# A gated cross-attention and mixture-of-experts kernel on one core: surplus branch in mid-stream, k of two batches at once, routing table in thirds

## The chip, the cores and the metric

The kernel runs on one core of a Trainium2 chip. The metric is the device time of one execution in microseconds (us), lower is better, as the median of several runs. All arithmetic is in 32-bit floats.

The core has five engines that each take their own instructions in order and meet over semaphores: PE (TensorE, matrix products; its weight loads are listed apart as PEld), DVE (VectorE), ACT (ScalarE), POOL (GpSimd) and SP (SyncE, which here only starts transfers). A "q" behind an engine's name (POOLq, PEldq) marks steps of its sequencer: branches, semaphores, register loads, drains.

## What is computed

Eight batches of 256 tokens with 256 features go through gated cross-attention (16 heads of 64, context of 120 rows) and then a gated mixture of eight experts of which each token takes two. Cut to what matters:

```python
x = x + tanh(g_xattn) * attention(layernorm(x), context)   # B=8, N=256, D=256, M=120
x = x + tanh(g_ffn) * moe(layernorm(x))

def attention(x, context):
    q = x @ w_q                      # 256 -> 16 heads x 64
    k, v = split(context @ w_kv)     # 256 -> 2 x 1024
    p = softmax(q @ k.T / 8)         # per head
    return (p @ v) @ w_out + b_out

def moe(x):                          # E=8 experts, DFF=1024
    probs = softmax(x @ Wr.T)
    top2 values, divided by their sum, are the gates
    return sum over the two experts e of gate_e * (silu(x @ W1[e].T) @ W2[e].T)
```

## The kernel before, in words

The order of instructions on PE, DVE, ACT and SP is written by hand: they are issued as the program's text runs (`tc.manual_schedule`), and each engine takes its own in that order. POOL does small arithmetic and the indirect transfers. Everything is one long straight stream with one branch at its end.

**Attention stage.** The loop runs over 32 units `(b, o, nb)`: a batch, one half of the heads, one half of the tokens; `k = 2*o + nb` counts the four units of a batch. In unit `s` PE takes, in this order: `scores` of the next unit (tile psc; DVE takes its maximum mx, ACT the exponentials pr), `weigh` (tile po, probabilities times v; in k=0 and k=2), `logits` (tile plT, and pl after it; the router's input, in k=1 of the odd batches from 3 on), one `project_q` for the next batch (pq), `project_k` (pk; k=1 and k=3), `wide_out` (pw; the output projection; k=1 for the first half of the batch before, k=2 for the second), `project_v` (pv; k=0 and k=3), and `turn_pr` (tr, the transposes of the unit's probabilities, which ACT copies into `pT_sb` and `weigh` reads). On DVE the copy of pk into kT comes first, then `divide` (probabilities by their sums) of the next unit, then the `router` (maximum, exponential on ACT, two picks, tally), then the sums of `wide_out`.

`project_k` makes k of one batch in two halves of four column blocks. Each matmul takes 120 columns of the context (one batch). psc has a single buffer; the projections share four PSUM buffers (`ps_mm`).

Two batches form a group of 512 tokens for routing. Each routed token's row (256 normalised features, its gates, its number) is sent by POOL's indirect transfers (L362) into a list per expert in DRAM, `routed`.

**Expert stage.** Tiles of 128 rows of one expert's list. First come eight tiles that are known to exist (`first`, one per expert, order 0, 1, 2, 6, 3, 4, 5, 7), then 23 `full` tiles whose expert and row are looked up in a table, and in steps 16 to 23 two `quad` tiles beside them, which mix the last rows of four experts. In step `i` PE does `go_up` of tile i (ph: 16 matmuls, ACT's SiLU behind it), the transposes of tile i+1 (`turn`, xtT, copied by DVE into xT), and `down` of tile i-1 (py: 8 matmuls; each 32-bit matmul has two records in the profile, and a weight load for each). DVE scales py by the gate into y (L856), and POOL adds y to the output by an indirect transfer (L873), each held until the one before has landed. For full tiles DVE also copies the expert's weights (L803, L812). SP loads rows four tiles ahead (L771, L791).

The last batch's output projection and routing lie in steps 1 to 4: `norm_y` and `norms_y.finish` (rows, L193), then `turn_y` (lnT_f, L203) at the head of step 2.

`table()` is a generator of small DVE steps on rows of up to 31 numbers: it finds for each full tile its row and expert (`full_row`, `expert_i`; L673 to L702), and then the same for quads (L705 to L751). It is run in two pieces, at the ends of steps 4 and 5:

```python
        if i == 4:
            parts = table()
            ...
        if 3 < i < 6:
            tables.append(next(parts))
```

**The branch.** The lists could be longer than 23 full and two quad tiles; for that the program ends with a conditional body (L1216 loads a count into a register of each engine, L1217 branches on it). For these inputs the count is zero and the body is jumped over.

The prologue (L119 to L165) makes constants on DVE and POOL, among them three for the table (`quarter_i`, `lane`, `places_q`; L140 to L151), while PE runs eleven idle matmuls (L1019).

Of the kernel before, what the change touches and what calls it, by code (L numbers as in the profile page):

```python
# [9 lines left out]
F32 = mybir.dt.float32  # L10
I32 = mybir.dt.int32
AF = mybir.ActivationFunctionType
ALU = mybir.AluOpType
AX = mybir.AxisListType

P = 128
B, N, D = 8, 256, 256
M = 120
# [8 lines left out]
DC = D // P  # L27
# [21 lines left out]
def tile_gated_xattn_moe(  # L49
# [74 lines left out]
    for e in range(E):  # L124
# [12 lines left out]
        places_q[:, QUADS:], [[1, 4 * QUADS]], base=0, channel_multiplier=0,  # L137
        allow_small_or_imprecise_dtypes=True,
    )
    quarter_i = const.tile([P, 1], I32, name="quarter_i")  # L140
    nc.vector.tensor_scalar(
        quarter_i, number[:, 0:1], 5, None, ALU.arith_shift_right
    )
    lane = const.tile([P, 1], F32, name="lane")
    nc.vector.scalar_tensor_tensor(
        lane, quarter_i, float(-QUARTER), number[:, 0:1], ALU.mult, ALU.add
    )
    for q in range(QUADS):
        nc.vector.tensor_scalar(
            places_q[:, q : q + 1], quarter_i, float(4 * q), None, ALU.add  # L150
        )  # L151
    octal = const.tile([P, E], F32, name="octal")
    for e in range(E):
        nc.vector.memset(octal[:, e : e + 1], float(E**e))
# [8 lines left out]

    minus_half = const.tile([P, 4], F32, name="minus_half")
    nc.gpsimd.memset(minus_half, -0.5)  # L165

    class Norms:

# [291 lines left out]

    kTs = {}

    def project_k(b, h):
        if h == 0:
            kTs[b] = ap.tile([P, IC, M], F32, tag="kT", name=f"kT_{b}")
        pk = ps_mm.tile([P, 512], F32, tag="mm", name=f"pk_{b}_{h}")
        for i in range(4):
            for c in range(DC):
                nc.tensor.matmul(
                    pk[:, ts(i, M)],  # L470
                    lhsT=wkv_sb[:, c, ts(4 * h + i, P)],
                    rhs=ctxT_sb[:, c, ts(b, M)],
                    start=(c == 0),
                    stop=(c == DC - 1),
                )
        return lambda: nc.vector.tensor_copy(
            kTs[b][:, ts(h, 4), :].rearrange("p c m -> p (c m)"), pk[:, : 4 * M]
        )

    def project_q(b, xnT, h):  # L480
# [188 lines left out]
    def table():  # L669

        rest_i = row("rest_i", E, I32)  # L673
        nc.vector.scalar_tensor_tensor(
            rest_i, count(NBLK, fw[2]), float(-P), bump, ALU.add, ALU.add
        )
        whole_i = row("whole_i", E, I32)
        nc.vector.tensor_scalar(whole_i, rest_i, 7, None, ALU.arith_shift_right)
        counts, begin = row("counts", 2 * E), row("begin", 2 * E)
        tails, whole = counts[:, :E], counts[:, E:]  # L680
        nc.vector.tensor_scalar(whole, whole_i, 1.0, None, ALU.mult)
        left = row("left", E)
        nc.vector.scalar_tensor_tensor(
            left, whole, float(-P), rest_i, ALU.mult, ALU.add
        )
        nc.vector.tensor_scalar(tails, left, float(P - QUARTER), None, ALU.is_gt)
        nc.vector.tensor_scalar(begin[:, E:], first_row, float(P), None, ALU.add)
        nc.vector.scalar_tensor_tensor(
            begin[:, :E], whole, float(P), begin[:, E:], ALU.mult, ALU.add
        )  # L690
        upto = summed("w", counts)

        at = row("at", FULLS)
        nc.vector.tensor_scalar(at, places_w, upto[:, 2 * E - 1 :], None, ALU.add)
        used = row("used_w", FULLS)
        nc.vector.tensor_scalar(used, at, 0.0, None, ALU.is_ge)
        which, first = sought("w", at, upto, counts, begin, P)
        full_row = row("full_row", FULLS, I32)
        where(first, used, full_row)
        expert_i = row("expert_i", FULLS, I32)  # L700
        nc.vector.tensor_scalar(used, which, float(E), float(-E), ALU.is_ge, ALU.mult)
        nc.vector.tensor_tensor(expert_i, which, used, ALU.add)  # L702
        yield expert_i, full_row

        quarters = row("quarters", E)  # L705
        nc.vector.tensor_scalar(quarters, left, 0.0, None, ALU.is_gt)
        for k in range(1, 3):
            nc.vector.scalar_tensor_tensor(
                quarters, left, float(k * QUARTER), quarters, ALU.is_gt, ALU.add
            )  # L710
        nc.vector.scalar_tensor_tensor(
            quarters, tails, -3.0, quarters, ALU.mult, ALU.add
        )
        upto_q = summed("q", quarters)
        used = row("used_q", 5 * QUADS)
        nc.vector.tensor_scalar(used, places_q, upto_q[:, E - 1 :], None, ALU.is_lt)
        which, first = sought("q", places_q, upto_q, quarters, begin[:, :E], QUARTER)
        where(first, used, first)
        nc.vector.tensor_scalar(which, which, float(E - 1), None, ALU.min)

        quad_row = row("quad_row", QUADS, I32)
        nc.vector.tensor_scalar(quad_row, first[:, :QUADS], lane, None, ALU.add)
        own = row("own", QUADS * E).rearrange("p (n e) -> p n e", e=E)
        eighth = row("eighth", QUADS)
        nc.vector.tensor_scalar(
            eighth, which[:, :QUADS], -1.0, float(E), ALU.mult, ALU.add
        )
        shape = [P, QUADS, E]
        nc.vector.tensor_tensor(
            own,  # L730
            rank.unsqueeze(1).to_broadcast(shape),
            eighth.unsqueeze(2).to_broadcast(shape),
            ALU.is_equal,
        )
        octets = which[:, QUADS:].rearrange("p (n e) -> p n e", e=E)
        nc.vector.tensor_tensor(
            octets, octets, octal.unsqueeze(1).to_broadcast([P, QUADS // 2, E]), ALU.mult
        )
        experts_i = row("experts_i", QUADS // 2, I32)
        with nc.allow_low_precision("whole numbers under 2**24, exact"):  # L740
            nc.vector.tensor_reduce(experts_i, octets, AX.X, ALU.add)

        more, more_i = row("more", 1), row("more_i", 1, I32)
        nc.vector.tensor_scalar(
            more, upto[:, 2 * E - 1 :], float(SPARE - FULLS), 0.0, ALU.add, ALU.max
        )
        more_q = row("more_q", 1)
        nc.vector.tensor_scalar(
            more_q, upto_q[:, E - 1 :], float(-4 * MIXED), 0.0, ALU.add, ALU.max
        )  # L750
        nc.vector.tensor_tensor(more_i, more, more_q, ALU.add)  # L751
        yield quad_row, own, experts_i, more_i
# [283 lines left out]
    for s, (b, o, nb) in enumerate(units):  # L1036
# [32 lines left out]
        elif n < B:  # L1069
            project_q(n, xnTs[n], k - 1)  # L1070
        if k == 1:
            if n < B:
                copies.append(project_k(n, 0))
            if routing and n < B:
                lg = next(lg)
            if b > 0:
                sums.append(wide_out(b - 1, 0, ps_mm))
            if routing and n == B:
                lg = next(lg)
        if k == 3:  # L1080
            if n < B:
                copies.append(project_k(n, 1))
            if b > 0:
                project_v(b, 1)
        for copy in copies:
            copy()
        if s + 1 < len(units):
# [13 lines left out]
        if n < B:  # L1101
            for step, each in list(sending.items()):
                if s < 8 * step + 18:
                    next(each)
        if b == 0 and k == 2:
            nc.vector.tensor_scalar(bias_sb, bias_sb, tg[:, 0:1], None, ALU.mult)
        if s in (3, 4):
# [34 lines left out]
    load_expert(5)  # L1142
    g = NG - 1
    for i, t in enumerate(order):
        w2_of = state["ready"][2][2]
        if i == 2:
            turn_y(B - 1, bank_tr)
# [22 lines left out]
            open_tile(order[i + 1], xts[i + 1])  # L1170
        if mixed:
            next(running)
        if i == 0:
            norms_y.finish()
            weigh(B - 1, 1, ps_py)
# [3 lines left out]
        if i == 3:  # L1179
            sending[g] = places(g, groups[g][0], picked[g], bank_tr)  # L1180
        w2 = w2_of()
        close_tile()
        state["pending"] = *new, w2
        if mixed:
            next(running)
        if i == 1:
            norms_y.finish()
        if i == 2:
            lg = next(lg)
            picked[g] = router(g, lg)  # L1190
# [5 lines left out]
                next(sending[g])  # L1196
        if i == 4:
            parts = table()
            routing_pool.close()
            qp.append(  # L1200
                ctx.enter_context(
                    tc.tile_pool(name="quads", bufs=1, side="right", reuse_waits="tile")
                )
            )
        if 3 < i < 6:
            tables.append(next(parts))
        while len(xts) <= min(i + AHEAD, len(order) - 1 if tables else 7):
            xts[len(xts)] = load(order[len(xts)])
# [3 lines left out]
            load_expert(3)  # L1212
            load_expert(7)
    close_tile()

    more = nc.values_load(tables[1][3][0:1, 0:1], min_val=0, max_val=FULLS)  # L1216
    with tc.If(more > 0):  # L1217
        spare = {}
        for j in range(SPARE):
            tj = ("full", j)  # L1220
            xt = load(tj)
            w1, gate, copy_w2 = weights(tj, xt)
            w2 = copy_w2()
            down(tj, up(tj, turn(tj, xt), w1), gate, xt, w2)
        for j in range(MIXED, QUADS):
            for _ in quad(j, load(("quad", j))):
                pass
        spare = None


# [41 lines left out]
```

## Time and profile before

| | |
|---|---|
| median of 3 runs | 548.06 us (547.97 to 548.73) |
| the profiled execution | 547.79 us; its span 546.0 us |
| mean granted PE clock | 0.991 |
| PE busy | 527.7 us (97% of the span) |
| DVE, ACT, POOL busy | 285.8, 219.5, 129.3 us |
| attention stage, to the first tile (PE, L832) | to 274.3 us |
| first tiles, last batch's routing, table | to about 336 us |
| full and quad tiles | to 531.8 us |
| tail, PE's last matmul to the end | 531.8 to 546.0 us |

Times below are microseconds from the span's start in that one execution. In the profile's lists an operation is named by line, engine and "output <- inputs"; "idle before <- releaser" says what ended the idle time of the engine ahead of it.

### The profile page before, as it was taken

Reading aid. Unit: us, or ns where it says so; the run is one execution under the profiler, and the core shown is the slowest. Engines: PE = TensorE matmul, PEld = TensorE weight load, DVE = VectorE, ACT = ScalarE, POOL = GpSimd, SP = SyncE. Lnnn points to the kernel's source line nnn. Section 1 sums busy time; section 2 is a strip of 40 time slices with the busy share of each in tenths; the row PEclk is TensorE's granted clock in tenths of the full one; section 3 lists DMA queues with packets and bytes.
Section 4 is the critical chain, followed back from the end, with each engine's and each line's share of the span. In section 5 each row is a group of like instructions: output and inputs, shape, how many; then the busy total and the mean of one; then the engine's idle time right before and its main releaser. Section 6 shows DMA issues by size and latency. Waiting matters only on the chain. (4 is left out here: it accounts for less than half of the span.)

```text
span 546.0 us, 10124 instructions
## 1 busy us (share of the span) xinstructions
PE 527.7 (97%) x3796; PEld 448.3 (82%) x3796; DVE 285.8 (52%) x683; ACT 219.5 (40%) x700; POOL 129.3 (24%) x135
## 2 busy tenths in 40 slices
PE   8999999999999999999999999999999999999990
PEld 7788878878788788887788999999988878799980
DVE  3676555567655676555563456444444444354420
ACT  1666465554555554646530311101146546311100
POOL 2021100101323013110024372222312134343421
PEclk9999999999999999999999999999999999999996
DMA  8999980410614101020099833221222121222220
GB/s 297 336 304 295 309 233 20 160 34 1 214 40 159 56 1 51 31 80 0 21 357 320 253 90 61 40 37 31 39 40 31 30 35 19 46 35 30 33 32 12
DMA packets 46439, 57.53 MB, mean 105 GB/s; under 512 B 3184, under 2 KB 41456, under 8 KB 46384
## 3 DMA queue, kind: packets, MB, share of 16 engines
q1 hardware_dynamic: 39488, 47.35, 28.5%
q0 software_dynamic: 6480, 8.81, 9.1%
q8 instruction: 32, 0.52, 0.4%
q10 hardware_dynamic: 416, 0.66, 0.4%
q14 instruction: 23, 0.19, 0.1%
HBM read 28.67 MB, written 28.27 MB: 104 GB/s over the span
## 5 line engine op out<-in xcount | busy, mean ns | idle before, releaser
L534 ACT ACTIVATE pr<-psc,mx 128x120 f32<-128x120 f32 x256 | 88.2, 371 | 64.1 <-DVE mx L528 64.1
L832 PEld LDWEIGHTS ph_full<-xT_full,w 128*128 128x128 f32 x736 | 85.1, 192 | 5.8 <-issue 5.0
L832 PE MATMUL ph_full<-xT_full,w 128*128 128x128 f32 x736 | 86.7, 276 | 0.0
L848 PE MATMUL py_full<-w,hT_full 128*128 128x256 f32 x368 | 83.1, 379 | 0.0
L848 PEld LDWEIGHTS py_full<-w,hT_full 128*128 128x128 f32 x368 | 68.3, 190 | 8.3
L873 POOL DMA_INDIRECT out_dram<-y_full,xt_full x23 | 39.7, 1726 | 101.0 <-DVE y_full L856 77.7
L484 PE MATMUL pq<-xnT,w_sb 128*128 128x256 f32 x256 | 62.7, 389 | 0.4 <-DVE xnT L204 0.4
L840 ACT ACTIVATE hT_full<-ph_full 128x1024 f32<-128x1024 f32 x23 | 23.5, 1022 | 97.0 <-PE ph_full L832 97.0
L578 PE MATMUL pw<-w_sb 128*128 128x256 f32 x256 | 58.6, 383 | 0.0
L522 DVE TENSOR_REDUCE mx<-psc 128x8 f32<-128x960 f32 x32 | 37.0, 1156 | 37.0 <-PE psc L514 36.9
L534 ACT ACTIVATION_READ_ACCUMULATOR pr<-psc,mx 128x1 f32 x256 | 55.5, 217 | 0.0
L484 PEld LDWEIGHTS pq<-xnT,w_sb 128*128 128x128 f32 x256 | 46.6, 190 | 10.7 <-issue 3.1
L578 PEld LDWEIGHTS pw<-w_sb 128*128 128x128 f32 x256 | 47.5, 190 | 8.7 <-issue 2.5
L362 POOL DMA_INDIRECT routed<-rows,slot x32 | 31.8, 992 | 56.4 <-DVE slot L358 49.4
L554 ACT COPY w_sb<-tr 120x512 f32<-120x512 f32 x64 | 34.6, 596 | 19.4 <-PE tr L553 19.4
L543 DVE TENSOR_TENSOR pr<-pr,sm 128x960 f32<-128x960 f32 x32 | 37.0, 1158 | 1.1
L514 PE MATMUL psc<-kT,w_sb 64*128 64x120 f32 x512 | 37.2, 284 | 0.0
L920 ACT COPY part<-w_sb 128x1024 f32 x32 | 31.1, 1044 | 14.1 <-PE py_q L959 13.5
L856 DVE TENSOR_SCALAR y_full<-py_full,gate 128x256 f32<-128x256 f32 x23 | 11.1, 484 | 48.5 <-PE py_full L848 44.8
L514 PEld LDWEIGHTS psc<-kT,w_sb 64*128 64x128 f32 x512 | 31.1, 187 | 6.4 <-issue 3.4
L553 PEld LDWEIGHTS tr<-ident,pr 128*120 128x120 f32 x256 | 29.5, 138 | 5.9 <-issue 4.3
L553 PE MATMUL tr<-ident,pr 128*120 128x128 f32 x256 | 33.5, 273 | 0.1
(174 smaller groups left out, 673.2 us busy)
## 6 DMA issues: line engine op xcount, KB each, us to landing
routed<-w_sb SPq DMA_DIRECT2D x8, 2120.0 KB, 21.6
w_sb<-in_w1T_dram SPq DMA_DIRECT2D x8, 1024.0 KB, 5.9
w_sb<-in_w2T_dram SPq DMA_DIRECT2D x8, 1024.0 KB, 9.2
xt_full<-routed SPq DMA_DIRECT2D x23, 132.5 KB, 2.1
out_dram<-x SPq DMA_DIRECT2D x8, 256.0 KB, 2.5
x<-in_x_dram SPq DMA_DIRECT2D x7, 256.0 KB, 2.7
w_sb<-in_w_kv_dram SPq DMA_DIRECT2D x3, 512.0 KB, 8.2
xt_first<-routed SPq DMA_DIRECT2D x8, 132.5 KB, 2.5
```

The lines of the kernel that those rows point to most:

```text
L362: send = nc.gpsimd.indirect_dma_start(out=routed[:, :], out_offset=bass.IndirectOffsetOnAxis(ap=slot[:, i : i + 1], axis=0), in_=rows[h][: ...
L484: nc.tensor.matmul(pq[:, i, :], lhsT=wq_sb[:, c, ts(2 * h + i, P)], rhs=xnT[:, c, :], start=(c == 0), stop=(c == DC - 1),)
L514: nc.tensor.matmul(psc[:, j, ts(i, M)], lhsT=qT[ts(j, DH), 4 * o + i, ts(nb, P)], rhs=kT[ts(j, DH), 4 * o + i, :], start=True, stop=True,)
L522: nc.vector.tensor_reduce(mx.rearrange("p (j i) -> p j i", i=4), psc[:, :, : 4 * M].rearrange("p j (i m) -> p j i m", m=M), AX.X, ALU.max,)
L534: nc.scalar.activation(pr[:, h, :], psc[:, j, ts(i, M)], AF.Exp, bias=mx[:, h : h + 1], scale=QK_SCALE, accum_out=sm[:, h : h + 1],)
L543: nc.vector.tensor_tensor(pr, pr, sm.unsqueeze(2).to_broadcast([P, 8, M]), ALU.mult)
L553: nc.tensor.transpose(tr[:M, i, :], pr[:, 4 * j + i, :], ident)
L554: nc.scalar.copy(pT_sb[:, ts(j, 4), ts(nb, P)], tr[:M, :, :])
L578: nc.tensor.matmul(pw[:, :D], lhsT=oT_sb[b % 2][:, ci, ts(k, P)], rhs=wo_sb[:, ci, :], start=(ci == 0), stop=(ci == IC - 1),)
L832: nc.tensor.matmul(ph[:, f, :], lhsT=w1[:, c, ts(f, P)], rhs=xT[:, c, :], start=(c == 0), stop=(c == DC - 1),)
L848: nc.tensor.matmul(py[:, :D], lhsT=hT[:, f, :], rhs=w2[:, f, :], start=(f == 0), stop=(f == FC - 1),)
L873: add = nc.gpsimd.indirect_dma_start(out=out[:, :], out_offset=bass.IndirectOffsetOnAxis(ap=slots[:, k : k + 1], axis=0), in_=y[own, :], i ...
```

## The change

Six edits:

- For batches 2 to 7, k is projected for two batches at once (`project_kk`): 240 columns per matmul, four matmuls per call, four calls per pair of batches. kT of the pair is one tile. The calls stand at the end of the unit's projections: for batches 2 and 3 in all four units of batch 1, for the later pairs in k=1 and k=3 of the two batches ahead of them. Batch 6 has none left. `project_k` stays for batches 0 and 1.
- The table is run in thirds: a new `yield` after L696; the pieces are run at the end of step 4, in step 5 ahead of `down`, and at the end of step 5. Row loads of full tiles so start one tile later.
- The eighth batch's normalised rows (`norms_y.finish` in step 1) are made ahead of `close_tile`, so ahead of that step's y.
- The three table constants are made in unit 7 rather than in the prologue.
- The count for the branch is loaded in step 8, and the branch with its body stands at the head of step 12, the 13th tile.

The diff, cut:

```diff
-    quarter_i = const.tile([P, 1], I32, name="quarter_i")
-    ...
+    def quarters_places():
+        ...
+    def open_k(b):
+        kk = ap.tile([P, IC, 2, M], F32, tag="kT", name=f"kT_{b}")
+        for i in range(2):
+            kTs[b + i] = kk[:, :, i, :]
+        kTs[b, 2] = kk
...
+    def project_kk(b, h):
+        if h == 0:
+            open_k(b)
+        pk = ps_mm.tile([P, 512], F32, tag="mm", name=f"pk_{b}_{h}")
+        for i in range(2):
+            for c in range(DC):
+                nc.tensor.matmul(
+                    pk[:, ts(i, 2 * M)],
+                    lhsT=wkv_sb[:, c, ts(2 * h + i, P)],
+                    rhs=ctxT_sb[:, c, ts(b // 2, 2 * M)],
+                    start=(c == 0),
+                    stop=(c == DC - 1),
+                )
+        return lambda: nc.vector.tensor_copy(
+            kTs[b, 2][:, ts(h, 2), :, :].rearrange("p c b m -> p (c b m)"),
+            pk[:, : 4 * M],
+        )
...
         used = row("used_w", FULLS)
         nc.vector.tensor_scalar(used, at, 0.0, None, ALU.is_ge)
+        yield
...
         if k == 1:
-            if n < B:
-                copies.append(project_k(n, 0))
+            if b == 0:
+                copies.append(project_k(1, 0))
             if routing and n < B:
                 lg = next(lg)
             if b > 0:
...
         if k == 3:
-            if n < B:
-                copies.append(project_k(n, 1))
+            if b == 0:
+                copies.append(project_k(1, 1))
             if b > 0:
                 project_v(b, 1)
+
+        if b == 1:
+            copies.append(project_kk(2, k))
+        elif 1 < b < 6 and k % 2 == 1:
+            copies.append(project_kk(2 * (b // 2) + 2, 2 * (b % 2) + k // 2))
         for copy in copies:
             copy()
...
+        if s == 7:
+            quarters_places()
...
     for i, t in enumerate(order):
+        if i == 12:
+            with tc.If(more > 0):
+                ...
+        if i == 8:
+            more = nc.values_load(tables[1][3][0:1, 0:1], min_val=0, max_val=FULLS)
...
+        if i == 5:
+            tables.append(next(parts))
...
         w2 = w2_of()
+        if i == 1:
+            norms_y.finish()
         close_tile()
         state["pending"] = *new, w2
         if mixed:
             next(running)
-        if i == 1:
-            norms_y.finish()
...
         if i == 4:
             parts = table()
+            next(parts)
...
-        if 3 < i < 6:
+        if i == 5:
             tables.append(next(parts))
...
     close_tile()
-    more = nc.values_load(tables[1][3][0:1, 0:1], min_val=0, max_val=FULLS)
-    with tc.If(more > 0):
-        ...
```

More of the change, by code (lines that the diff above doesn't have):

```diff
@@ L139, in tile_gated_xattn_moe @@
     )
-    quarter_i = const.tile([P, 1], I32, name="quarter_i")
[L141 to L151, printed above, removed]
     octal = const.tile([P, E], F32, name="octal")
@@ L165, in tile_gated_xattn_moe @@
     nc.gpsimd.memset(minus_half, -0.5)
+    lane = const.tile([P, 1], F32, name="lane")
+    def quarters_places():
+        quarter_i = small.tile([P, 1], I32, tag="quarter_i", name="quarter_i", bufs=1)
+        nc.vector.tensor_scalar(
+            quarter_i, number[:, 0:1], 5, None, ALU.arith_shift_right
+        )
+        nc.vector.scalar_tensor_tensor(
+            lane, quarter_i, float(-QUARTER), number[:, 0:1], ALU.mult, ALU.add
+        )
+        for q in range(QUADS):
+            nc.vector.tensor_scalar(
+                places_q[:, q : q + 1], quarter_i, float(4 * q), None, ALU.add
+            )
     class Norms:
@@ L461, in tile_gated_xattn_moe @@
     kTs = {}
+    def open_k(b):
[3 more added lines that the diff above has]
+        kTs[b, 2] = kk
     def project_k(b, h):
-        if h == 0:
-            kTs[b] = ap.tile([P, IC, M], F32, tag="kT", name=f"kT_{b}")
+        if b == h == 0:
+            open_k(0)
         pk = ps_mm.tile([P, 512], F32, tag="mm", name=f"pk_{b}_{h}")
@@ L476, in project_k @@
         return lambda: nc.vector.tensor_copy(
-            kTs[b][:, ts(h, 4), :].rearrange("p c m -> p (c m)"), pk[:, : 4 * M]
+            kTs[b][:, ts(h, 4), :], pk[:, : 4 * M].rearrange("p (c m) -> p c m", m=M)
+        )
+    def project_kk(b, h):
[10 more added lines that the diff above has]
+                    stop=(c == DC - 1),
+                )
+        return lambda: nc.vector.tensor_copy(
+            kTs[b, 2][:, ts(h, 2), :, :].rearrange("p c b m -> p (c b m)"),
+            pk[:, : 4 * M],
         )
@@ L1144, in tile_gated_xattn_moe @@
     for i, t in enumerate(order):
+        if i == 12:
+            with tc.If(more > 0):
+                spare = {}
+                for j in range(SPARE):
+                    tj = ("full", j)
+                    xt = load(tj)
+                    w1, gate, copy_w2 = weights(tj, xt)
+                    w2 = copy_w2()
+                    down(tj, up(tj, turn(tj, xt), w1), gate, xt, w2)
+                for j in range(MIXED, QUADS):
+                    for _ in quad(j, load(("quad", j))):
+                        pass
+                spare = None
+        if i == 8:
+            more = nc.values_load(tables[1][3][0:1, 0:1], min_val=0, max_val=FULLS)
         w2_of = state["ready"][2][2]
@@ L1214, in tile_gated_xattn_moe @@
     close_tile()
-    more = nc.values_load(tables[1][3][0:1, 0:1], min_val=0, max_val=FULLS)
[L1217 to L1228, printed above, removed]
 def kernel(**inputs):
```

## The prediction

> **What bounds the kernel now.** I read the busy shares first, then what PE waited for, then the timeline of one routing batch, then the end. The page:
>
> ```profile
> PE 527.7 (97%) x3796; PEld 448.3 (82%) x3796; DVE 285.8 (52%) x683; ACT 219.5 (40%) x700; POOL 129.3 (24%) x135
> ...
> PE   8999999999999999999999999999999999999990
> ```
>
> PE is busy in every slice but the last, and the granted clock is full (9) up to there. So PE's order of work sets the time, and a microsecond counts only if it is PE work, a PE wait, or time behind PE's last matmul. The view of PE's waits is the whole list of what PE ever waited for:
>
> ```profile
> PE idle L1019 <- POOL ones L119: 1.9, 1, 1.9
> PE lnT_f L203 <- DVE rows L193: 1.0, 1, 1.0
> PE ph_first L832 <- DVE xT_first L825: 0.6, 1, 0.6
> PE pq L484 <- DVE xnT L204: 0.4, 1, 0.4
> ```
>
> There are 3.9 us to win from waits and no wait at all inside the attention batches. How near to one they are shows the timeline of batch 3, unit k=1, where a router stands (columns: start, busy time, engine and line; PE's pl at 124.57, pw from 124.68 to 128.13, and DVE's divide at 125.57 lie in the gaps):
>
> ```profile
> 122.79 1.94 PE L469 MATMUL pk<-ctxT_sb,w_sb 128*128 128x120 f32 x16
> 122.86 0.26 DVE L224 COPY lgT<-plT 128x128 f32<-128x128 f32 x1
> ...
> 124.77 0.66 DVE L476 COPY kT<-pk 128x480 f32<-128x480 f32 x1 [1.66 <-PE pk L469]
> ...
> 127.09 0.23 ACT L262 ACTIVATE p<-p 128x32 f32<-128x32 f32 x1 [1.79 <-DVE p L261]
> ...
> 128.83 1.07 ACT L554 COPY w_sb<-tr 120x512 f32<-120x512 f32 x2 [1.50 <-PE tr L553]
> ...
> 130.18 1.95 PE L563 MATMUL po<-w_sb 120*64 120x256 f32 x16
> ```
>
> To be seen: pk (1.8 us of PE) covers the copy of lgT before pl; the kT copy, the divide and the router's start follow on DVE behind pk; and ACT's copies of tr end at 129.90, 0.28 us before PE's po needs them. The last lines belong to the end: POOL's last scatter in the timeline, then the view of line 1217, the branch, and that of line 1268, the end of the program (durations in ns: shortest, median, longest).
>
> ```profile
> 533.61 1.54 POOL L873 DMA_INDIRECT out_dram<-y_full,xt_full  x1 [2.96 <-DVEq L1217]
> ```
>
> ```profile
> L1217 ACTq COMPARE_BRANCH  x1: 50/50/50, 525.5 to 525.5; - x1
> L1217 PEldq COMPARE_BRANCH  x1: 3457/3457/3457, 528.3 to 528.3; - x1
> ...
> L1217 POOLq INC_SWDGE_SEM  x1: 1648/1648/1648, 537.4 to 537.4; - x1
> ```
>
> ```profile
> L1268 POOLq DRAIN  x3: 46/107/6036, 539.1 to 545.7; - x3
> ```
>
> PE's last matmul ends at 531.76 and the span at 546.0: 14.2 us of tail, in which the last scatter lands at 537.40, the INC runs to 539.05, the long DRAIN from 539.08 to 545.11, and 0.84 us of closing steps follow.
>
> **Part by part**, against the profiled execution of 547.79 us (the median of the three runs, 548.06, lies 0.27 above).
>
> *k of two batches at once.* For batches 2 to 7, 96 matmuls of 120 columns become 48 of 240. Pitch of one: eight of 120 columns from 122.79 to 124.57, 0.2225 us; four of 256 (pq, 100.88 to 102.61), 0.4325; two of 512 (pv, 108.27 to 109.98), 0.855, which is 0.00167 per column. Between them 240 columns cost 0.4055, a group of four 1.62 against 1.78: 0.16 saved in each of 12 groups, **-1.9**. Ends: -0.6 if 240 costs what 256 does, -2.1 by the per-column figure of 512. The Trainium skill speaks of the same: "TensorE: Matmul & The Clock Gate", Back-to-back issue gap, gives about 81 ns for a load and matmul of 128 columns and 131 ns for 512; by that ratio (an estimate, a straight line between) 240 columns would cost only 1.18 times 120, and the part would save 8.8 us. The rows here give 1.94 times for 256 against 120, and they are taken.
>
> *Where the joint k stands.* The group now comes after pw in PE's order, and in routing batches pl follows directly on pq. In k=1 of batches 3 and 5: (a) pl is reached at 122.79 but lgT is copied only by 123.12 (DVE does mx and the statistics first), with the handover +0.45. (b) pw then runs to 126.80 and the group to 128.42. The kT copy stands ahead of the divide and the router on DVE, so it starts 0.2 later, at 128.62, instead of 124.77. The divide ends at 130.6, and the router's exp on ACT runs at about 130.95 to 131.2 instead of 127.09. ACT takes its work in order: the two copies of tr stand behind that exp, and end at about 132.25. PE, 0.29 later than before (0.45 - 0.16), wants po at 130.5: a wait of 1.7, where the margin was 0.28. (c) The rest of the router (3.7 us, 127.35 to 131.03 before) keeps DVE to about 135, so mx of the next unit and its exps come some 4 us later, half of it taken back by PE's own wait; ACT's copies are still late at the next unit or two, for which I take 0.6, between 0 and 1.2. Sum 2.75 for each batch, **+5.5** for two. Ends: +2.7 if half of it is absorbed, +7.5 if DVE's lag hits psc as well, whose one buffer must be read by the exps first. Batch 7's router stood behind pw already and does not change.
>
> *Batch 6 has no k work left*: its units k=1 and k=3 lose 1.78 us each. k=3 is then 1.1 psc + 1.73 pq + 1.71 pv + 1.0 tr = 5.5 us of PE, against the chain psc to mx (0.2), mx and its scaling (1.4), eight exps of 0.34 (2.75) and handovers of 0.1 to 0.3, about 5.3. Two or three waits of 0.3: **+0.7** (0 to 1.4). Batch 1, which takes the groups of batches 2 and 3 in all its four units, only gets longer ones.
>
> *Eighth batch's rows ahead of a result.* At i=1 DVE does y (295.35) first, then rows (295.75 to 296.5), and lnT_f waits 0.99. rstd is ready at 293.95, so the rows can be done by 294.7; PE wants them at 295.31. **-1.0** (to 0). y becomes no later, since DVE idles 2.2 us ahead of it.
>
> *Table in thirds.* Before, the first part (320.58 to 327.67) held xT_first back: PE waited 0.60 at 328.06. Now the part up to L696 runs at i=4 (to 322.80), xT follows its transposes at once and that wait goes. L629 to L702 (4.92 us, 322.75 to 327.67) then stand behind it, and at i=5 y comes first, then the last third from L706 to L751 (5.84, plus 0.3 to y's start), ahead of the next xT. I get 329.3 for the second third's end, 335.4 for the last's, 335.8 for xT, and PE wants it at 334.8: a new wait of 1.06. Net **+0.5** (-0.6 to +1.1). The xt loads, which need full_row, start one tile later (about 329; a load lands in 2.1 us) and are needed at 339.
>
> *Table constants later*: eight small DVE steps, 1.15 us busy, leave the prologue. PE's idle matmuls run to 6.8 us and cover most of it: **-0.1** (-0.4 to 0). At unit 7 DVE has idle time for them.
>
> *The branch.* The load of its condition at i=8 costs each engine 0.27 to 0.51 (the TENSOR_LOADs of line 1216) of sequencer time. At i=12 each engine waits for its own earlier work and jumps; SP and POOL also wait for their transfers to land. What is queued behind: on PE tile 12's up, which waits only for an xT and hT from before the branch; on DVE w1 of tile 13; on SP the xt loads, four tiles ahead; on POOL the scatters. POOL is the slowest: tile 10's scatter lands some 4.3 us after the branch, the INC takes 1.65, so it is free at 6.0, and the next y comes at 8. DVE ends its y 0.8 after PE's branch; if it then pays a fetch as ACT did before (2.44 to its next step at 527.98), it copies w1 (1.23), gate (0.14) and xT_13 (0.42) by 5.5, gaps included, and PE wants xT_13 one tile later (7.25 us), at 7.8. On PE itself the COMPARE_BRANCH took 3.46 us before with a 16 KB fetch inside (529.32 to 530.38), but its sequencer stood 4.0 us ahead of its matmuls (18 records of 0.217 queued), so the queue covers it; what remains is the drained queue, event and first weight load: **+0.55** (0.4 to 2.4, the end being ACT's uncovered fetch). The skill, "Runtime: NRT & Kernel Launch", Instruction fetch mechanics, says that a taken branch whose target lies outside the window stalls until the page is fetched, which speaks against a branch in mid-stream. ACT's and PE's rows agree, DVE's 0.6 (532.20 to its next step at 532.80) does not; without PE's cover the rule would make this part about 3.5 us.
>
> *The tail.* The INC goes from the end. Nothing then stands between the last scatter's end on POOL (535.16) and DRAIN: 535.16 + 6.04 + 0.84 = 542.0 instead of 545.95, **-3.9**. Ends: -1.7 if DRAIN starts only when the scatter has landed (537.40); -6.9 if DRAIN was long only because of the INC, when SP's twelve semaphore waits (0.74) close at 537.40 + 0.74 + 0.84 = 539.0. Nothing in this trace shows a DRAIN without an INC; I take the middle, as DRAIN starts 1.7 us after the last landing here and still takes 6 us, so it does not seem to wait for data.
>
> Sum: -1.9 + 5.5 + 0.7 - 1.0 + 0.5 - 0.1 + 0.55 - 3.9 = +0.35, so 548.14 profiled and **548.4** for the median. 0.2%, about what this kernel's measurement can tell from no change, is 1.1 us: 546.96 to 549.16 counts as no change.
>
> **Rivals.**
> 1. *Slower: DRAIN waits for the landing.* Place: POOL, behind the last scatter. Price: DRAIN starts at 537.40 instead of 535.16, +2.24: **550.6**. It is slower than 549.16 from a start after 535.9 on. For: POOL's INC itself began exactly at the landing. Against: the 6 us behind it.
> 2. *Faster: DRAIN shrinks without the INC.* **545.4** (548.4 - 3.0). For: the other two DRAINs of POOL take 0.05 and 0.11. Against: the INC had ended before it.
> 3. *Faster: the routing stalls are half*, because PE's lateness feeds back and (c) vanishes while the handovers in (b) are shorter: 548.4 - 2.75 = **545.6**. Against: a margin of 0.28 against an exp 3.9 us later.
> 4. *The jump is not covered on PE*: 1.9 us to 2.9 us more, about **550.8**.
>
> **How the numbers follow.** Forecast 0.45, spread 547.0 to 550.0 by the errors of its terms: 0.05 faster, 0.27 the same, 0.13 slower. Rival 1: 0.20, slower. Rival 2: 0.17, faster. Rival 3: 0.15, faster. Rival 4: 0.03, slower. Faster 0.37, same 0.27, slower 0.36. The range runs from 544.3, the lower part of rivals 2 and 3 (both together, 542.6, are left out), to 551.3, the upper part of rivals 1 and 4. The likeliest case's own range is 547.0 to 550.0.
>
> **What the profile after would show.** Right: PE waits "po <- ACT" of about 1.7 us in batches 3 and 5 and "pl <- DVE" of 0.4; no wait at lnT_f; a wait of about 1 us at an up of the last first tile; a PE gap of about half a microsecond ahead of the 13th tile; POOL's long DRAIN directly behind the last scatter and a tail of some 10 us. Wrong: attention batches without PE waits (rival 3); a tail of 12.5 us (rival 1) or 7.3 us (rival 2); a hole of over 2 us at the branch (rival 4); or 240 columns at a pitch under 0.39 or over 0.43 us.

## The result and the profile after

The changed kernel takes 546.72 us (median of 8 runs, 546.43 to 547.57) against 548.14 (8 runs, 547.92 to 548.73): a ratio of 0.9974, 95% interval 0.9963 to 0.9985. That is 1.4 us faster, a small gain where no change (+0.3) was forecast. The profiled execution took 546.83 us, its span is 545.13 (545.95 before).

The answering lines of the page of the changed kernel, and the whole list of what its PE waited for:

```profile
PE 528.0 (97%) x3700; PEld 445.5 (82%) x3700; DVE 282.5 (52%) x683; ACT 219.6 (40%) x700; POOL 128.7 (24%) x135
...
PE   8999999998999999999999999999999999999992
```

```profile
PE po L593 <- ACT w_sb L584: 2.6, 3, 1.2
PE idle L1050 <- POOL ones L119: 2.0, 1, 2.0
PE ph_first L863 <- DVE xT_first L856: 0.9, 1, 0.9
PE pl L230 <- DVE lgT L227: 0.6, 2, 0.3
PE pq L514 <- DVE xnT L207: 0.4, 1, 0.4
PE ph_full L863 <- PEq L1185: 0.3, 1, 0.3
```

The wait at lnT_f (1.0 before) is gone. That of the seventh first tile's up (0.6 before) is gone too, and the eighth tile's up now waits 0.9. New are three waits of po for ACT, two of pl for DVE, and a short one at the branch (PEq, line 1185). PE's busy time hides the saved k matmuls, because the list counts a wait only in part: the po of batch 3 shows 1.16 us of idle time and is busy for 2.43 us instead of 1.95, and by the starts it loses 1.70. More exact are the starts of the same step in both traces, after minus before:

| step on PE | after minus before, us | step change |
|---|---|---|
| first scores | +0.19 | +0.19 |
| scores ahead of batch 3's router | +2.80 | k of two batches moved ahead (about 3.3), less 0.165 for each group |
| scores two units later | +4.84 | +2.04 in batch 3 |
| the same in batch 5 | +4.35, then +6.40 | +2.05 |
| batch 6 without k, and its sequel in batch 7 | +6.23, then +3.50 | two times -1.78, then +0.83 |
| up of the first tile | +3.50 | |
| up of the third, behind lnT_f | +2.28 | -1.22 |
| ups of the seventh, eighth and ninth (table) | +1.51, +2.48, +2.59 | -0.77, +0.97, +0.11 |
| ups of the 13th and 14th (branch) | +3.05, +3.12 | +0.53 in all from +2.59 |
| last up | +3.12 | 0 |

So PE ends 3.12 us later than before, and the span ends 0.82 us earlier: the tail is 3.94 us shorter (10.25 against 14.19). The unit that was shown for batch 3, in the timeline of the changed kernel:

```profile
125.65 0.26 DVE L227 COPY lgT<-plT 128x128 f32<-128x128 f32 x1
126.06 0.30 PE L230 MATMUL pl<-ident,lgT 128*128 128x128 f32 x1 [0.30 <-DVE lgT L227]
126.19 3.62 PE L608 MATMUL pw<-w_sb 128*128 128x256 f32 x16
...
129.65 1.78 PE L498 MATMUL pk<-ctxT_sb,w_sb 128*128 128x240 f32 x8
...
131.47 0.66 DVE L505 COPY kT<-pk 128x480 f32<-128x480 f32 x1 [5.56 <-PE pk L498]
...
133.79 0.23 ACT L265 ACTIVATE p<-p 128x32 f32<-128x32 f32 x1 [5.68 <-DVE p L264]
133.93 1.05 ACT L584 COPY w_sb<-tr 120x512 f32<-120x512 f32 x2
...
134.54 2.43 PE L593 MATMUL po<-w_sb 120*64 120x256 f32 x16 [1.16 <-ACT w_sb L584]
```

DVE sits idle for 5.56 us until the joint group is done, the router's exp is 3.9 us later in the unit than before, ACT's copies of tr stand directly behind it, and PE's po waits for them. All of it is as (a) and (b) of the working had it. The group itself runs from 129.65 to 131.27, 1.62 us for four matmuls of 240 columns.

For (c), what the lag does behind that wait, these lines of the same timeline count, the mx of the next two units and the copies of tr with the po that reads them:

```profile
138.03 1.15 DVE L552 TENSOR_REDUCE mx<-psc 128x8 f32<-128x960 f32 x1
...
145.56 1.15 DVE L552 TENSOR_REDUCE mx<-psc 128x8 f32<-128x960 f32 x1
...
150.92 1.15 ACT L584 COPY w_sb<-tr 120x512 f32<-120x512 f32 x2
...
152.29 1.95 PE L593 MATMUL po<-w_sb 120*64 120x256 f32 x16
```

The same copies and po in the timeline of the kernel before:

```profile
145.81 1.07 ACT L554 COPY w_sb<-tr 120x512 f32<-120x512 f32 x2
...
147.61 1.95 PE L563 MATMUL po<-w_sb 120*64 120x256 f32 x16
```

The first mx comes 5.80 us behind the start of its scores (132.24), where it came 2.24 behind them before: DVE is 3.56 us late. The second comes 2.01 behind instead of 1.20, so 0.81 late, and of the third nothing is left (1.35, as in the first experiment below, which has no such lag). The copies of tr end at 152.07, 0.22 us ahead of po; before, they ended 0.73 us ahead of it. So the lag reaches ACT there, takes 0.5 us of a margin of 0.7, and PE does not wait. In batch 5 the margin goes from 0.73 to 0.13.

The tail and the branch, in the timeline (the last scatter, and PE's matmuls around the branch) and in the views of the branch's line and of the program's end:

```profile
536.71 1.55 POOL L904 DMA_INDIRECT out_dram<-y_full,xt_full  x1 [2.93 <-issue]
```

```profile
L1185 PEldq COMPARE_BRANCH  x1: 3399/3399/3399, 370.6 to 370.6; - x1
...
L1185 POOLq INC_SWDGE_SEM  x1: 1044/1044/1044, 380.9 to 380.9; - x1
```

```profile
370.76 3.62 PE L879 MATMUL py_full<-w,hT_full 128*128 128x256 f32 x16
...
374.68 3.59 PE L863 MATMUL ph_full<-xT_full,w 128*128 128x128 f32 x30 [0.30 <-PEq L1185]
```

```profile
L1311 POOLq DRAIN  x3: 46/113/7814, 536.5 to 544.9; - x3
```

The INC now lies at 381, and PE's starts from the 14th up on stay at +3.12. The DRAIN is issued at 536.49, beside the last scatter, and ends at 544.30, which is 6.04 us behind that scatter's end at 538.26, and not behind its landing (540.54). The closing steps take 0.8 more. PE's COMPARE_BRANCH takes 3.40 us (3.46 at the end before), from 370.56 to 373.96, while PE's matmuls already queued run on to 374.38, so the matmuls lose only 0.53.

### The profile page after: what moved, and what is told of

It reads as the page before. It is cut to its first block, busy times and chain, and to the rows that moved or that the text cites. A ratio compares the mean times of both kernels' runs of the same rounds, so it can differ in the third digit from the quotient of the medians.

```text
span 545.1 us, 9935 instructions
## 1 busy us (share of the span) xinstructions
PE 528.0 (97%) x3700; PEld 445.5 (82%) x3700; DVE 282.5 (52%) x683; ACT 219.6 (40%) x700; POOL 128.7 (24%) x135
## 5 line engine op out<-in xcount | busy, mean ns | idle before, releaser
L593 PE MATMUL po<-w_sb 120*64 120x256 f32 x256 | 32.7, 386 | 2.6 <-ACT w_sb L584 2.6
```

The lines of the kernel that those rows point to most:

```text
L593: nc.tensor.matmul(po[ts(j, DH), k, :], lhsT=v_sb[b % 2][:, ts(2 * (4 * o + i) + j, DH)], rhs=pT_sb[:, 4 * j + i, :], start=True, stop=True,)
```

## The experiments

Two theories stood at the start. The first: every term works as forecast, only the carry-on of the router's lag (the term (c), 0.6 for each routing batch) does not exist, so the place of the joint k group is what costs, and the branch is what pays. The second: the terms are not independent; the edits depend on one another, and the sum came out near zero by other ways.

**The group ahead of pl and pw.** Edit against the changed kernel:

```diff
         if k == 1:
             ...
+            if 1 < b < 6:
+                copies.append(project_kk(2 * (b // 2) + 2, 2 * (b % 2)))
             if routing and n < B:
                 lg = next(lg)
...
-        elif 1 < b < 6 and k % 2 == 1:
-            copies.append(project_kk(2 * (b // 2) + 2, 2 * (b % 2) + k // 2))
+        elif 1 < b < 6 and k == 3:
+            copies.append(project_kk(2 * (b // 2) + 2, 2 * (b % 2) + 1))
```

> The joint k group of unit k=1 goes back to where k stood before: behind pq and ahead of pl and pw (batches 2 to 5); everything else as in the changed kernel. Theory A (the place of the group, not its width, costs time): in the trace of the changed kernel PE loses 0.50 at pl and 1.70 at po in each of batches 3 and 5, 4.4 us in all; with 1.62 us of k ahead of pl, lgT is copied in time, the kT copy, the divide and the router's exp start some 3.5 us earlier, and the copies of tr are no longer held. Expected 546.7 - 4.4 = 542.3 us, no PE wait at pl or po in batches 3 and 5. Theory B (a group of 240 columns with a kT copy that serves two batches is itself late, wherever it stands): the waits move or stay, 545 to 547 us.

Measured: 542.80 us (ratio to before 0.9897, 0.9883 to 0.9912). Of PE's waits in the batches only one is left (view of PE's waits, the one of batch 7):

```profile
PE po L593 <- ACT w_sb L584: 0.3, 1, 0.3
```

The scores two units behind the routers start 2.2 us earlier in each of the two batches, 4.4 us together, as expected. The medians differ by 3.9; in the trace the branch costs 0.68 here instead of 0.53 and the tail is 0.2 longer. Its profiled execution lost 1.0 us at the start to a weight load that came late (pk waited for the transfer of w_kv), which has to do with no edit. The place is the cost, not the width.

**k as before.** Edit: `project_k` and its two calls as in the kernel before; `project_kk` and `open_k` go.

> The changed kernel with k of one batch at a time, in the old place; the other five edits stay. Theory A (the k edit alone is a loss: 12 groups save 0.165 us each, 1.95 in all, and waits of 4.4 in batches 3 and 5 and 0.8 in batch 7 go against it): 546.7 - 3.3 = 543.4 us, with the first tile's up at the time of the kernel before. Theory B (the edits overlap, so that a wait elsewhere takes the difference): 545 us or more.

Measured: 543.36 us (0.9908, 0.9895 to 0.9921). PE's last up starts 3.35 us earlier than in the changed kernel. The k edit as made was a loss of 3.4 us; in the better place it is a gain of 0.6 (542.80 against 543.36). Of the 1.95 that its matmuls save, batch 7's wait of 0.83 takes part; the traces show the 1.12 that is left in the attention stage, and 0.15 more at the branch and 0.1 more in the tail against it, and the rest is not placed.

**The branch back at the end.** Edit: the load of the count and the branch with its body moved from steps 8 and 12 behind the loop.

> The changed kernel with the load of the count and the branch back at the end of the program. Theory A (the branch in mid-stream costs PE 0.5 us and takes 4.0 us from the tail): 546.7 + 3.5 = 550.2 us, the tail behind PE's last matmul 14.2 us again with INC_SWDGE_SEM in it. Theory B (the tail was shorter for another reason, as the program's length or the time at which POOL ends): under 548 us.

Measured: 550.87 us (1.0044, 1.0030 to 1.0057), and the up of the 14th tile 0.54 us earlier against the steps ahead of it. POOL again goes through its INC (540.20 to 541.84) and then its DRAIN, 6.036 us from 541.88 on. The span is 3.6 us longer than the changed kernel's, as forecast (3.5); the medians differ by 4.2, and the other half microsecond lies outside the span, its cause open.

**The table in two pieces.** Edit: the new `yield` goes and the pieces run as before.

```diff
-        yield
...
-        if i == 5:
-            tables.append(next(parts))
...
-            next(parts)
...
-        if i == 5:
+        if 3 < i < 6:
             tables.append(next(parts))
```

> The changed kernel with the table in two pieces as before. Theory A (thirds took 0.77 us from one first tile's up and gave 0.97 and 0.11 to the next two): 546.7 - 0.3 = 546.4 us, the wait of the last first tile's up gone and 0.6 back at the one before. Theory B (thirds are worth something, because loads or the branch profit): 547 us or more.

Measured: 546.56 us (0.9969, 0.9958 to 0.9981) against 546.72: thirds and halves can't be told apart. In its trace the 0.61 at the earlier up is back and the later wait is gone, 0.31 us to the good, and the branch then costs 0.84 instead of 0.53. That is not the table's doing: in a second profile of the changed kernel itself (below) the branch costs 0.79, and over all profiles with the branch in mid-stream 0.53 to 0.84.

**The branch alone.** Edit: the kernel before, with the count loaded in step 8 and the branch ahead of step 12.

> The kernel before with the branch edit alone: count loaded in step 8, branch ahead of step 12. Theory A (the tail gives 4.0 us, the branch in mid-stream costs PE 0.5, nothing depends on the other edits): 548.1 - 3.5 = 544.6 us. Theory B (part of the gain needs the later loads of the other table split): 545.5 or more.

Measured: 544.47 us (0.9935, 0.9922 to 0.9948). PE loses 0.54 there, the tail gives the rest. One of the six edits is worth two and a half times what all six are together.

**The last third of the table a step later.** Edit: in step 6 behind the copy of xT, instead of at the end of step 5.

```diff
-        if i == 5:
+        if 4 < i < 7:
             tables.append(next(parts))
...
-        if i == 5:
-            tables.append(next(parts))
```

> The changed kernel with the last third of the table moved from the end of step 5, ahead of the last first tile's xT copy, to step 6, behind that copy; there the 5.8 us of small DVE steps delay only the y of that step. Theory A (the 0.97 + 0.11 us that PE loses at the up of steps 7 and 8 come from that place): 546.7 - 1.1 = 545.6 us, no wait at the up of a first tile. Theory B (y late by some 2 us holds a PSUM buffer or the next w1 copy): a wait moves to the up of the first full tile, 546.5 us or more.

Measured: 546.12 us (0.9973, 0.9959 to 0.9987), with a wide spread of its runs (545.49 to 550.12). The forecast was 545.6. Its profile shows another thing, which may be why the spread is wide: in step 5 DVE and ACT both resumed at 330.8, though PE's matmuls they waited for ended at 325.9 and 326.1, and PE's next up waited 1.7 (called the late release below). That step is the same program as in the changed kernel. Behind it PE does gain 1.07 us over the changed kernel, as expected.

**Both together.** The group ahead of pl and pw, and the last third of the table in step 6.

> The joint k group ahead of pl and pw, and the last table third in step 6, together. If both gains are independent: 542.8 - 1.1 = 541.7 us; if not, 542.8.

Measured: **541.17 us** (0.9873, 0.9858 to 0.9887), the best version, so the two gains do not take from each other (1.6 below the first of them alone, where 1.1 was expected; 0.3 of the rest are branch and tail, which differ that much between profiles). Only these waits are left on PE:

```profile
PE idle L1050 <- POOL ones L119: 1.9, 1, 1.9
PE pq L514 <- DVE xnT L207: 0.4, 1, 0.4
PE ph_full L863 <- PEq L1187: 0.3, 1, 0.3
PE po L593 <- ACT w_sb L584: 0.3, 1, 0.3
```

**The copies of tr ahead of the router.** Edit:

```diff
-        if routing and n < B and k == 1:
-            picked[g] = router(g, lg)
-        for add in sums:
+        for add in sums if k != 1 else []:
             add()
...
         turn_pr((b, o, nb), *prs.pop(s))
+        if routing and n < B and k == 1:
+            picked[g] = router(g, lg)
+        for add in sums if k == 1 else []:
+            add()
```

> The changed kernel, the joint group still behind pw, but in units k=1 of batches 3 and 5 the copies of tr stand ahead of the router (its exp on ACT, its DVE steps, and the sums behind them) in the written order; PE's order is the same. Theory A (po waits because ACT's copies of tr are queued behind the router's exp): the po wait goes, 1.7 us in each of two batches, only pl's 0.5 each stays: 546.7 - 3.4 = 543.3 us. Theory B (it is DVE that is late, and a wait on it stands behind the one on ACT): po or pp waits for DVE instead, 545.5 to 546.7 us.

Measured: 551.26 us (1.0050, 1.0024 to 1.0076; runs from 546.72 to 554.23). Its profile has the same late release in step 5, by 4.9 us, and two waits of a first tile's up of 1.7 and 3.6 us behind it, which have nothing to do with the edit; its attention stage is 0.25 us shorter than the changed kernel's. So it was run again, beside the changed kernel:

> The changed kernel once more, beside the next run, to see whether the hold of about 5 us that three kernels showed between the up of step 5 and DVE's and ACT's next work belongs to a program or to an occasion. If to the program: 546.7 us and no such hold here.

> The kernel with the copies of tr ahead of the router once more. Its attention stage showed 0.9 us less wait at po and 0.7 us of new wait for DVE at pp in batch 3, so 0.1 to 0.3 us less in all than the changed kernel; its time was 4.5 us longer because ACT and DVE resumed some 5 us late in step 5. If that hold belongs to the program: again 550 us or so; if to the occasion: 546.5 us.

Measured: the changed kernel 547.06 us (0.9977, 0.9963 to 0.9991), this one 546.60 (0.9971, 0.9957 to 0.9985), with no late release in either profile. The late release does not belong to the program's text. The edit itself is worth at most 0.3 us, not 3.4: theory B holds. In batch 3 (view of PE's waits from 120 to 150 us) po waits no more, but

```profile
PE pp L317 <- DVE w_sb L600: 0.6, 1, 0.6
PE pl L230 <- DVE lgT L227: 0.3, 1, 0.3
```

PE meets DVE's lag 7 us further on instead, at 141.46. By the starts of the scores PE loses 0.87 us less over that unit than in the changed kernel and 0.68 more two units on: there ACT's copies of tr end at 152.31, later than the po that begins with the first of them at 151.87, so here the late copies do cost PE time.

**More lag.** Edit: behind the router in batches 3 and 5

```diff
+            spent = small.tile([P, GB, E], F32, tag="spent", name=f"spent_{g}")
+            for _ in range(16):
+                nc.vector.tensor_scalar(
+                    spent, rank.unsqueeze(1).to_broadcast([P, GB, E]), 1.0, None, ALU.mult
+                )
```

> The changed kernel with 16 more small DVE steps (0.2 us each, about 3.4 us) behind the router in unit k=1 of batches 3 and 5. In the trace of the changed kernel the router's lag on DVE (mx of the next unit comes 4 us later than before) cost nothing beyond the waits at pl and po: the forecast's extra 0.6 for each batch was not there. Theory A (PE's wait at po and DVE's lag are the same microseconds, the lag is used up by the time of po and there is no further slack): the added lag comes through for the most part, at pp or the next psc, 2 to 3 us for each batch, 551 to 553 us. Theory B (DVE has slack of several us in these units, the lag would have been absorbed anyway): under 0.5 for each batch, about 547 us.

Measured: 556.0 us (1.0141, 1.0121 to 1.0161), above theory A's 551 to 553. The added steps keep DVE busy for 3.42 us in each batch. PE loses 3.2 us more than in the changed kernel in batch 3 and 4.4 in batch 5, where 2 to 3 were expected; most of the new waits are for DVE (view of PE's waits):

```profile
PE po L593 <- ACT w_sb L584: 2.8, 4, 1.2
...
PE pq L514 <- DVE x L615: 1.8, 2, 0.9
PE pp L317 <- DVE w_sb L600: 1.3, 2, 1.0
PE pc L285 <- DVE w_sb L600: 1.0, 1, 1.0
```

So the changed kernel's lag had used up what slack there was: what is added comes through about in full.

**No last scatters.** Edit: `add_up` is not called for the last four tiles.

> The changed kernel without the scatter-adds of the last four tiles (their sums are left out of the output). Theory A (POOL's long drain is 6.04 us counted from the end of POOL's last transfer, and is at the end only because that transfer is): POOL drains while PE still works, and the program ends about 1.5 us behind PE's last matmul: a span near 536.5, 538.2 us. Theory B (a fixed 6 us of the program's end, whatever POOL did before): 544 us or more.

Measured: 541.29 us (0.9867, 0.9832 to 0.9901), between the two theories, with the late release of step 5 in its profile and a spread from 538.12 to 543.01; the fastest run is at theory A's forecast. The view of the program's end carries the verdict:

```profile
L1312 POOLq DRAIN  x3: 46/113/7257, 520.0 to 541.0; - x3
```

The long DRAIN starts at 520.0 beside the last scatter left and is over at 527.3, 5.7 us behind that scatter, while PE works on until 539.7. The span ends 1.5 us behind PE. So the DRAIN costs time because POOL's last scatter ends behind PE's last matmul, in the changed kernel by 3.4 us.

## Why the prediction was wrong

The forecast was +0.35 us for the profiled execution; the two profiled executions differ by -0.96 and the medians by -1.4. Of the 1.3 us between forecast and profile, 1.1 are one part, the place of the joint k group.

- **k of two batches: right.** 0.405 per matmul was forecast, 1.62 us for four is what the trace has; 12 groups save 0.165 each, 1.98 us. Measured are 1.82 times 120 columns for 240 (0.405 against 0.2225). The figures of the Trainium skill ("TensorE: Matmul & The Clock Gate", Back-to-back issue gap), with a straight line between them (an estimate), would have made it 1.18 times; the measurement decides.
- **Where the group stands, (a) and (b): right.** 0.50 at pl (0.45 forecast) and 1.70 at po (1.7 forecast) in each of the two batches.
- **(c), the carry-on, is the step that failed.** Forecast were 0.6 for each batch, as a wait for ACT's copies of tr at the next unit or two; measured is nothing: from the second scores behind the router to the next router the difference between the traces only falls, by 0.165 for each k group. The lag is there (mx 3.56 us late, about the 4 of the working), and the copies of tr do come late at the next po, by 0.5 us in batch 3 and 0.6 in batch 5. But that po had 0.73 us to spare in the kernel before, and the rows of the profile before show it (copies to 146.88, po at 147.61); the working charged the lateness as a wait without holding it against this margin. PE's wait of 1.70 and the idle time that DVE had ahead of mx in those units (0.96 and 0.40 us in the trace before, none now) take back 3.1 of the 3.56 us. How near it was is shown by two kernels: with the copies of tr ahead of the router the wait comes back at pp, for DVE, and two units on at po, and with more lag what is added comes through. Term (c) was 1.2 us too high for two batches, (a) 0.1 too low; that is the 1.1, and with it the sign.
- **Batch 6 without k: right in size**, +0.83 against +0.7, but not in its place: units k=1 and k=3 of batch 6 gain their 1.78 us each in full, and there is one wait, at po in the first unit of batch 7. The working's own numbers, 5.5 us of PE against a chain of 5.3, would have given no wait in batch 6; that the sum is near is in part luck. Its statement that there is no wait inside the attention batches also passes over pq's 0.4, which lies in batch 0 and is unchanged.
- **Rows ahead of y: right**, -1.22 against -1.0. The table in thirds: the two waits are as forecast (-0.77 and +1.08 against -0.6 and +1.06), but halves with the same rest take the same time. Table constants (-0.1 forecast): not to be seen; the first scores differ by 0.19 between traces, and by as much (0.21) in the kernel whose prologue was not changed.
- **Branch: right**, +0.53 against +0.55. The matmuls that PE has queued cover its COMPARE_BRANCH of 3.40 us but for this. The Trainium skill ("Runtime: NRT & Kernel Launch", Instruction fetch mechanics) says that a taken branch to a page outside the window waits until it is fetched; it gives no length. The 3.40 us step agrees with a stall, the 0.53 us that it costs PE do not come near the 3.5 that the working put on it without cover.
- **Tail: right**, -3.94 against -3.9. DRAIN's end fits a count from the end of the last scatter on POOL, as the middle case had it; rivals 1 (it waits for the landing) and 2 (it shrinks without the INC) are both refuted by its end at 538.26 + 6.04. Rival 3 (stalls half) names the right place and has (c) vanish, but (b) was as long as forecast: the stalls were 2.2 of 2.75 for each batch.

A sum of large terms of both signs that ends near zero has a sign that hangs on its smallest doubtful term; mine leaned on a term that had not been held against its row.

## What to carry to other kernels

A lag of an engine costs where it is longer than the margin of the step that needs it: behind the first wait that it causes, read the margin at each further such step, and charge only what goes beyond it (here 0.5 late against 0.7 to spare, nothing). When work is fused, look first at what stood behind the old, smaller step as cover and as supplier: here a group in a later place cost more than twice what it saved, and moving it back ahead of pl and pw gave 3.9 us. The end of this program belongs to POOL, whose last step has the longest closing work, so what stood there and was not needed there (the branch with its INC) was better put where queued work covers it: 3.94 us of tail for 0.5 to 0.8 on PE.

## What the runs showed of the hardware

POOL's closing DRAIN ended about 6 us behind the last indirect transfer or INC on POOL: 6.04 behind the scatter in the changed kernel, 6.07 behind the INC, and 5.7 behind the scatter where that lay ahead of PE's last matmul.

In four profiles (the late table, both together, the first run with the copies ahead, and that without last scatters) DVE and ACT resumed 2 to 5 us behind the matmuls that they waited for, in one and the same place of the program, in step 5. In the late-table kernel, matmuls that ended at 325.93 and 326.14 raised their semaphore at 330.75 and 330.79, in a burst with a third at 330.95, while PE's records run on. The same program text had it in one profile and not in another, and of four kernels run side by side one had it. Its cause stays open.
